# First attention of a Perceiver kernel: blocks taken in pairs, one set of two-bank PSUM tiles, the mask applied on GpSimd after the exponential

## The chip, the cores and the metric

The kernel runs on one core of a Trainium2 chip. The metric is the device time of one execution in microseconds. Before the change it is 784.37 us, the median of three runs (783.34 to 786.42). All times below are microseconds unless marked otherwise.

## What is computed

The network has two layers. A latent array `x` of 128 rows by 256 columns attends to a context of 12,544 rows by 256 columns. Layer 0 is a cross-attention with 4 heads of 64, a gated delta net, and a mixture of experts; layer 1 is a cross-attention with 16 heads of 16 over the same context, a linear attention with decay, and a second mixture of experts. The change is in the first cross-attention and in the loads around it. Cut to that, the reference is:

```
h = layernorm(x)
q = (h @ Wq)                    # 4 heads of 64
k, v = split(context @ Wkv)     # 12544 rows, 4 heads of 64 each
attn = softmax(where(mask, q @ k.T * 64**-0.5, -inf))   # per head, 128 x 12544
x = x + (attn @ v) @ Wo
```

The data are f32, the mask is one byte per entry.

## The kernel before, in words

The context comes in 25 blocks, 24 of 512 rows and one of 256 (`BLOCKS`). All of it stays in SBUF, one tile per block, for layer 1 uses it again. `xattn0_first` (L352) does the first attention. The scores are computed transposed, with the context rows on the partitions, so that the weights need no turning before they are multiplied with the values. One shift per query and head, `nm`, taken from the maximum over the first block, stands in for the running maximum. A second version (`xattn0`, L161), with a running maximum, is executed only when a sum of weights falls out of range; it is not in the executions shown here.

Per block there are four pieces of TensorE work, in an order that is written by hand (`manual_schedule(engines={PE})`, L365; the other engines' orders are made by the scheduler):

- `keys` (L389): for each half m of the 256 key columns, two products of 128x512 into a one-bank PSUM tile `pk`, and a ScalarE copy into `kT` (L399).
- `values` (L401): for each pair of 128-row chunks, four products of 128x256 into a one-bank tile `pv`, and a ScalarE copy into `v` (L412).
- `scores` (L415): per pair of chunks, GpSimd turns the mask bytes into 0 or -1e30 (`mb`, L423) and adds the shift (`shift`, L428); TensorE computes eight products into a two-bank tile `st` (L437); VectorE adds `e = st + shift` (L443), ScalarE takes the exponential in place (L444), VectorE adds e to the running `sums` (L445).
- `weigh` (L448): per e, eight products of v and e into the accumulator `ot` (L455).

In the profile each f32 product shows as two instructions, so a block has 8 `pk`, 16 `pv`, 32 `st` and 32 `ot` instructions.

[...]two tiles of two banks for `st`, three of one bank for everything else (`ps_mm`, L363), one for `ot`. The loop of L502 runs over blocks b: load block b+2, `keys(b)`, `values(b)`, `weigh(b - 1)`, `scores(b)`. After it come six pieces of `filler`, which is work of layer 1's attention (keys and values of the same context, L990 and L1006) used wherever TensorE would wait, and the last `weigh`. The total of filler work is fixed; what is not used in one place is used in a later one.

Ahead of the loop (L461 to L500) stand `keys(0)`, the layer norm of x (L137; its reciprocal root needs two table loads of ScalarE), the query product `pq` (L467) with its scaled copies, the plain scores `sc` of block 0 (L481) with their row maxima on VectorE (L484), `values(0)`, `keys(1)`, and the product `pn` (L495) that spreads the maxima, copied to `nm` (L496).

The loads: SP's queue issues x (L92), Wkv (L368), context block 0, Wq, the mask rows of block 0 (`m0`), block 1, and then blocks and masks as the loop asks for them. GpSimd's queue issues `row`, `col`, the two routers' weights, Wk and Wv of layer 1 (L94, L96, L1489, L1514, L1517) and Wo, with `turned` (L1495, L1496) computed from `row` between them.

Of the kernel before, what the change touches and what calls it, by code (L numbers as in the profile page):

```python
# [11 lines left out]
F32 = mybir.dt.float32  # L12
BF16 = mybir.dt.bfloat16
I32 = mybir.dt.int32
U8 = mybir.dt.uint8
# [56 lines left out]
def network(ctx: ExitStack, tc: tile.TileContext, a: dict, y_out, bad):  # L72
# [18 lines left out]
    x = act.tile([S, D], F32, tag="x", name="x_in")  # L91
    nc.sync.dma_start(x, a["x"])  # L92
    row = const.tile([128, NROW], F32, name="row")
    nc.gpsimd.dma_start(row, a["row"].partition_broadcast(128))  # L94
    col = const.tile([128, NCOL], F32, name="col")
    nc.gpsimd.dma_start(col, a["col"])  # L96
# [21 lines left out]
    def load_ctx(b):  # L118
        r, n = BLOCKS[b]
        nc.sync.dma_start(  # L120
            ctx_blocks[b], a["ctxT"][:, r : r + n].rearrange("(k p) n -> p k n", p=128)
        )
# [229 lines left out]
    def xattn0_first(x, ahead, ok, filler):  # L352
# [4 lines left out]
        with (  # L357
            tc.tile_pool(name="x0_w", bufs=1) as wp,
            tc.tile_pool(name="x0_kv", bufs=2) as kvp,
            tc.tile_pool(name="x0_e", bufs=3) as ep,  # L360
            tc.tile_pool(name="x0_s", bufs=2) as sp,
            tc.tile_pool(name="x0_st", bufs=2, space=PSUM) as ps_st,
            tc.tile_pool(name="x0_mm", bufs=3, space=PSUM) as ps_mm,  # L363
            tc.tile_pool(name="x0_ot", bufs=1, space=PSUM) as ps_ot,
            tc.manual_schedule(engines={PE}),  # L365
        ):
            wkv = wp.tile([128, KC, 2 * D], F32, name="wkv")
            nc.sync.dma_start(wkv, a["L0_xattn_Wkv"].rearrange("(k p) n -> p k n", p=128))  # L368
            load_ctx(0)
            wq = weights(a["L0_xattn_Wq"], D)  # L370
            m0 = sp.tile([S, 512], U8, tag="m0", name="m0", bufs=1)
# [7 lines left out]
            zl = wp.tile([1, 128], BF16, name="zl")  # L379
            nc.gpsimd.memset(zl, 0.0)  # L380
            zr = wp.tile([1, 256], BF16, name="zr")
            nc.gpsimd.memset(zr, 0.0)
# [5 lines left out]

            def keys(b):  # L389
                n = BLOCKS[b][1]  # L390
                kTs[b] = kvp.tile([128, 2, 512], F32, tag="kT", name="kT")[:, :, :n]
                for m in range(2):
                    pk = ps_mm.tile([128, 512], F32, tag="mm", name="pk")
                    for k in range(KC):
                        nc.tensor.matmul(  # L395
                            pk[:, :n], wkv[:, k, m * 128 : (m + 1) * 128], ctx_blocks[b][:, k, :],
                            start=(k == 0), stop=(k == KC - 1),
                        )
                    nc.scalar.copy(kTs[b][:, m, :], pk[:, :n])  # L399

            def values(b):  # L401
                vs[b] = kvp.tile([128, 4, D], F32, tag="v", name="v")
                for c0 in range(0, BLOCKS[b][1] // 128, 2):
                    pv = ps_mm.tile([128, 2, D], F32, tag="mm", name="pv")
                    for c in range(2):
                        rows = slice((c0 + c) * 128, (c0 + c + 1) * 128)
                        for k in range(KC):
                            nc.tensor.matmul(  # L408
                                pv[:, c, :], ctx_blocks[b][:, k, rows], wkv[:, k, D:],
                                start=(k == 0), stop=(k == KC - 1),  # L410
                            )
                    nc.scalar.copy(vs[b][:, c0 : c0 + 2, :], pv)  # L412


            def scores(b):  # L415
                r, n = BLOCKS[b]
                msk = sp.tile([128, 512], U8, tag="msk", name="msk", bufs=3)[:, :n]
                nc.sync.dma_start(msk, a["maskT"][:, r : r + n])
                es[b] = []
                for c0 in range(0, n // 128, 2):  # L420

                    mb = sp.tile([128, 2, S], F32, tag="mb", name="mb")
                    nc.gpsimd.tensor_scalar(  # L423
                        mb, msk[:, c0 * 128 : (c0 + 2) * 128].rearrange("p (c s) -> p c s", c=2),
                        BIG, BIG, ALU.mult, ALU.subtract,
                    )
                    shift = sp.tile([128, 4, 2, S], F32, tag="shift", name="shift")
                    nc.gpsimd.tensor_add(  # L428
                        shift, mb.unsqueeze(1).to_broadcast([128, 4, 2, S]),
                        nm.unsqueeze(2).to_broadcast([128, 4, 2, S]),  # L430
                    )
                    st = ps_st.tile([128, 4, 2, S], F32, tag="st", name="st")
                    for m in range(2):
                        for c in range(2):
                            for q in range(2):
                                rows = slice(q * DH, (q + 1) * DH)
                                nc.tensor.matmul(  # L437
                                    st[:, 2 * q + m, c, :],
                                    kTs[b][rows, m, (c0 + c) * 128 : (c0 + c + 1) * 128], qT[rows, m, :],
                                    start=True, stop=True,  # L440
                                )
                    e = ep.tile([128, 4, 2, S], F32, tag="e", name="e")
                    nc.vector.tensor_add(e, st, shift)  # L443
                    nc.scalar.activation(e, e, AF.Exp)  # L444
                    nc.vector.tensor_add(sums, sums, e)  # L445
                    es[b].append(e)
# [14 lines left out]
            keys(0)  # L461
            hT = layernorm(x, ps_mm, "mm")
            qT = wp.tile([128, 2, S], F32, name="qT")
            for m in range(2):
                pq = ps_mm.tile([128, 512], F32, tag="mm", name="pq")
                for k in range(KC):
                    nc.tensor.matmul(  # L467
                        pq[:, :S], wq[:, k, m * 128 : (m + 1) * 128], hT[:, k, :],
                        start=(k == 0), stop=(k == KC - 1),
                    )  # L470
                nc.scalar.mul(qT[:, m, :], pq[:, :S], DH**-0.5)


            mb0 = sp.tile([S, 512], F32, tag="mb0", name="mb0", bufs=1)
            nc.gpsimd.tensor_scalar(mb0, m0, BIG, BIG, ALU.mult, ALU.subtract)
            mx = sp.tile([S, 4], F32, tag="mx", name="mx")
            for m in range(2):
                sc = ps_st.tile([S, 2, 512], F32, tag="st", name="sc")
                for q in range(2):
                    rows = slice(q * DH, (q + 1) * DH)  # L480
                    nc.tensor.matmul(sc[:, q, :], qT[rows, m, :], kTs[0][rows, m, :], start=True, stop=True)  # L481
                for q in range(2):
                    t = ep.tile([128, 1024], F32, tag="e", name="t")[:, :512]
                    nc.vector.tensor_tensor_reduce(  # L484
                        out=t, in0=sc[:, q, :], in1=mb0, scale=1.0, scalar=-BIG,
                        op0=ALU.add, op1=ALU.max, accum_out=mx[:, 2 * q + m : 2 * q + m + 1],
                    )
            values(0)
            keys(1)
# [4 lines left out]
            pn = ps_mm.tile([128, 4, S], F32, tag="mm", name="pn")  # L494
# [5 lines left out]
            nc.tensor.matmul(ot.rearrange("p m s -> p (m s)"), zl, zr, start=True, stop=False)  # L500

            for b in range(NB):  # L502
                if b + 2 < NB:
                    load_ctx(b + 2)
                if b in ahead:
                    ahead[b]()
                if b > 1:
                    keys(b)
                if b > 0:
                    values(b)  # L510
                    weigh(b - 1, False)
                scores(b)
            filler.into(ps_mm, "mm")
            filler.fill(6)
# [3 lines left out]
            pl = ps_mm.tile([128, 2, S], F32, tag="mm", name="pl")  # L518
# [15 lines left out]
            po = ps_mm.tile([128, 512], F32, tag="mm", name="po")  # L534
# [497 lines left out]
    def weigh1(x, qs, kss, cp, sp, loaded, late):  # L1032
# [4 lines left out]
        with (  # L1037
# [4 lines left out]
            nc.vector.tensor_add(xb, x, row[:S, ROW["bv"]])  # L1042

# [443 lines left out]
    for n, r in enumerate(("L0_ffn_router_w", "L1_ffn_Wg")):  # L1487
        t = const.tile([128, KC, NE], F32, name=f"wr{n}")
        nc.gpsimd.dma_start(t, a[r].rearrange("(k p) n -> p k n", p=128))  # L1489
        wr.append(t)  # L1490
# [4 lines left out]
    nc.gpsimd.tensor_scalar_mul(turned[:, :NE], row[:, ROW["bg"]], -1.0)  # L1495
    nc.gpsimd.tensor_scalar(turned[:, NE:], row[:, ROW["iota"]], -1.0, 64.0, ALU.mult, ALU.add)  # L1496
# [17 lines left out]
    nc.gpsimd.dma_start(wk1, a["L1_xattn_Wk"].rearrange("(k p) n -> p k n", p=128))  # L1514

    wv1 = const.tile([128, KC, D], F32, name="wv1")
    nc.gpsimd.dma_start(wv1, a["L1_xattn_Wv"].rearrange("(k p) n -> p k n", p=128))  # L1517
# [26 lines left out]
    with tc.tile_pool(name="k1", bufs=3) as kp:  # L1544
        filler = Filler(kp)
        if bad is not None:
            ok0 = const.tile([128, 1], F32, name="ok0")
            x = xattn0_first(x, ahead, ok0, filler)
        else:
            x = xattn0(x, ahead)  # L1550
# [128 lines left out]
```

## Time and profile before

| What | us |
|---|---|
| the profiled execution, its own time | 784.51 |
| its span | 782.6 |
| head: 0 to the first transposed scores at 28.0, TensorE busy | 18.1 of 28.0 |
| blocks 0 and 1, 28.0 to 49.7, TensorE busy | 19.0 of 21.7 |
| blocks 2 to 24, 49.7 to 287.6, TensorE busy | 237.9 of 237.9 |
| rest of layer 0, 287.6 to 480, TensorE busy | 189.2 of 192.4 |
| layer 1's attention, 480 to 740, TensorE busy | 258.5 of 260.0 |
| the last layers, 740 to the end, TensorE busy | 27.3 of 42.6 |

The engines are called PE (TensorE), PEld (TensorE's weight loads, which overlap its products), DVE (VectorE), ACT (ScalarE), POOL (GpSimd) and SP. A line of a chain of waits or of a timeline begins with the start and the length in us, then the engine, the source line (in a timeline), the operation, what is written and from what, and how many instructions are taken together. What stands in brackets is the idle time of the engine just before, and what ended it. The busy time of TensorE contains modelled ends of pipelined products, and the times of several instructions together are from the first start to the last end.

### The profile page before, as it was taken

The page shows a single profiled execution, that of the slowest core. Times are in us where ns is not written, and L with a number is a line of the kernel's source. Part 1 is how long each engine was busy: PE and PEld are TensorE (multiplying, and loading weights), DVE is VectorE, ACT ScalarE, POOL GpSimd, SP SyncE. Part 2 cuts the span into 40 slices and gives each one's busy share as a digit, 9 for nine tenths or more (in the row PEclk, how much of TensorE's full clock was granted, in tenths as well). Part 3 has the DMA queues.
Part 4 walks back from the last instruction along what each step waited for, and adds up shares of the span by engine and source line. Part 5 has one row for each costly group of instructions (what it writes and reads, how often), then busy time and mean ns, then how long its engine had stood idle before and what let it go on. Part 6 is the DMA issues. An engine that isn't in the chain of part 4 may idle for free.

```text
span 782.6 us, 23795 instructions
## 1 busy us (share of the span) xinstructions
PE 749.9 (96%) x10821; PEld 558.0 (71%) x10821; DVE 250.5 (32%) x406; ACT 411.2 (53%) x540; POOL 246.4 (31%) x193
## 2 busy tenths in 40 slices
PE   4999999999999999999999999999999999999965
PEld 2667777777777776756668756667888888888852
DVE  0465445654466453983113133000000000000044
ACT  2244334433443334474224533336999999999940
POOL 6597677666776630416012011000000000000000
PEclk9999999999999999999999999999999999999988
DMA  9584000000000002233111345221442222222000
GB/s 291 213 280 172 9 8 4 8 8 8 7 6 6 2 15 84 85 117 123 58 44 41 106 128 134 78 81 58 121 115 74 68 58 74 68 58 72 4 1 12
DMA packets 35742, 56.70 MB, mean 72 GB/s; under 512 B 5760, under 2 KB 11952, under 8 KB 35632
## 3 DMA queue, kind: packets, MB, share of 16 engines
q1 hardware_dynamic: 35232, 54.00, 21.7%
q8 instruction: 87, 1.43, 0.8%
q0 software_dynamic: 400, 1.09, 0.5%
q14 instruction: 23, 0.19, 0.1%
HBM read 42.09 MB, written 12.98 MB: 70 GB/s over the span
## 4 chain that ended last, share of the span: by engine, by line
PE 90%; DVE 3%; ACT 2%; POOL 1%; issue 1%; DMA 1%; SPq 0%; ACTq 0%; DVEq 0%; POOLq 0%
PE st L1067 14%; PE ot L1084 12%; PE pk L395 11%; PE pv L1016 10%; PE pv L408 10%; PE pk L995 10%; PE st L437 6%; PE ot L455 6%; DVE acc L612 1%; DMA ctx<-in_ctxT 1%; POOL shift L428 1%; PE pr L602 1%; PE py L924 1%; PE py L1425 1%; PE pg L732 1%
## 5 line engine op out<-in xcount | busy, mean ns | idle before, releaser
L1073 ACT ACTIVATE e<-st 128x512 f32<-128x512 f32 x196 | 189.7, 1021 | 17.1 <-PE st L1067 15.7
L428 POOL TENSOR_TENSOR shift<-mb,nm 128x1024 f32<-128x1024 f32 x49 | 120.7, 2464 | 73.7 <-DVE e L443 59.3
L1067 PE MATMUL st<-qs,ks 32*128 32x128 f32 x3136 | 115.8, 283 | 0.8 <-ACT e L1073 0.8
L1067 PEld LDWEIGHTS st<-qs,ks 32*128 32x128 f32 x3136 | 96.9, 186 | 21.4 <-ACT e L1073 20.9
L444 ACT ACTIVATE e<-e 128x1024 f32<-128x1024 f32 x49 | 51.8, 1057 | 101.5 <-DVE e L443 100.0
L1084 PE MATMUL ot<-e,ctx 128*17 128x128 f32 x3136 | 104.7, 274 | 0.0
L395 PE MATMUL pk<-ctx,wkv 128*128 128x512 f32 (+1 forms) x200 | 93.7, 613 | 9.3 <-DMA ctx<-in_ctxT 9.3
L443 DVE TENSOR_TENSOR e<-st,shift 128x1024 f32<-128x1024 f32 x49 | 57.9, 1220 | 113.5 <-PE st L437 105.2
L995 PE MATMUL pk<-ctx,wk 128*128 128x512 f32 (+1 forms) x200 | 92.8, 591 | 1.3 <-ACT ctx L1021 1.3
L1016 PE MATMUL pv<-wv,ctx 128*128 128x256 f32 x392 | 92.8, 382 | 0.9 <-ACT kh L1002 0.9
L408 PE MATMUL pv<-wkv,ctx 128*128 128x256 f32 x392 | 89.2, 380 | 1.6 <-ACT kT L399 1.6
L408 PEld LDWEIGHTS pv<-wkv,ctx 128*128 128x128 f32 x392 | 74.2, 190 | 22.3 <-issue 10.0
L445 DVE TENSOR_TENSOR sums<-sums,e 128x1024 f32<-128x1024 f32 x49 | 87.8, 1792 | 4.8 <-ACT e L444 1.2
L1016 PEld LDWEIGHTS pv<-wv,ctx 128*128 128x128 f32 x392 | 72.8, 190 | 20.4 <-issue 10.0
L1084 PEld LDWEIGHTS ot<-e,ctx 128*17 128x17 f32 x3136 | 77.5, 97 | 11.9 <-ACT e L1073 0.3
L423 POOL TENSOR_SCALAR mb<-msk 128x256 f32<-128x256 uint8 x49 | 72.2, 1474 | 4.2
L395 PEld LDWEIGHTS pk<-ctx,wkv 128*128 128x128 f32 x200 | 37.1, 195 | 48.4 <-issue 45.4
L1113 DVE RECIPROCAL den<-pt 128x16 f32<-128x16 f32 x1 | 0.3, 257 | 208.7 <-PE pt L1110 208.7
L1002 ACT ACTIVATE kh<-pk,col 128x512 f32<-128x512 f32 (+1 forms) x50 | 33.9, 678 | 59.0 <-PE pk L995 58.8
L995 PEld LDWEIGHTS pk<-ctx,wk 128*128 128x128 f32 x200 | 36.1, 190 | 31.5 <-issue 26.5
L1021 ACT COPY ctx<-pv 128x512 f32<-128x512 f32 x49 | 28.7, 587 | 54.3 <-PE pv L1016 54.2
L412 ACT COPY v<-pv 128x512 f32<-128x512 f32 x49 | 28.6, 586 | 54.3 <-PE pv L408 54.3
(322 smaller groups left out, 620.3 us busy)
## 6 DMA issues: line engine op xcount, KB each, us to landing
ctx<-in_ctxT SPq DMA_DIRECT2D x24, 512.0 KB, 8.4
kd<-kh SPq DMA_DIRECT2D x48, 256.0 KB, 2.0
ks<-kd SPq DMA_DIRECT2D x192, 64.0 KB, 2.8
w<-in_L_ffn_expert_w SPq DMA_DIRECT2D x4, 512.0 KB, 3.7
ctx<-in_L_ffn_We SPq DMA_DIRECT2D x4, 512.0 KB, 4.7
msk<-in_maskT SPq DMA_DIRECT2D x24, 64.0 KB, 1.9
w<-in_L_attn_Wqk SPq DMA_DIRECT2D x2, 768.0 KB, 9.7
w<-in_L_attn_Wv SPq DMA_DIRECT2D x2, 768.0 KB, 5.1
```

The source lines that it names most:

```text
L395: nc.tensor.matmul(pk[:, :n], wkv[:, k, m * 128 : (m + 1) * 128], ctx_blocks[b][:, k, :], start=(k == 0), stop=(k == KC - 1),)
L408: nc.tensor.matmul(pv[:, c, :], ctx_blocks[b][:, k, rows], wkv[:, k, D:], start=(k == 0), stop=(k == KC - 1),)
L423: nc.gpsimd.tensor_scalar(mb, msk[:, c0 * 128 : (c0 + 2) * 128].rearrange("p (c s) -> p c s", c=2), BIG, BIG, ALU.mult, ALU.subtract,)
L428: nc.gpsimd.tensor_add(shift, mb.unsqueeze(1).to_broadcast([128, 4, 2, S]), nm.unsqueeze(2).to_broadcast([128, 4, 2, S]),)
L443: nc.vector.tensor_add(e, st, shift)
L444: nc.scalar.activation(e, e, AF.Exp)
L445: nc.vector.tensor_add(sums, sums, e)
L995: nc.tensor.matmul(pk, wk1[:, k, m * 128 : (m + 1) * 128], ctx_blocks[b][:, k, :], start=(k == 0), stop=(k == KC - 1),)
L1016: nc.tensor.matmul(pv[:, c, :], ctx_blocks[b][:, k, rows], wv1[:, k, :], start=(k == 0), stop=(k == KC - 1),)
L1067: nc.tensor.matmul(st3[:, j - 1, g, :] if j else st1[:, 0, g, :], kss[b % 3][r, g // 2, g % 2, c * 128 : (c + 1) * 128], qs[r, g, :], star ...
L1073: nc.scalar.activation(e[:, j].rearrange("p j g s -> p (j g s)"), st.rearrange("p j g s -> p (j g s)"), AF.Exp,)
L1084: nc.tensor.matmul(ot[32 * j : 32 * j + DH + 1, g, :], v[:, c, 8 * (g // 2) + 2 * j + g % 2, :], e[:, j, g, :], start=False, stop=(i + 1 = ...
```

## The change

1. Blocks are taken two at a time. For a pair the loop does `values` and `add_up` of the two blocks before, `keys` of both new ones, `weigh` of the two before, and `scores` of both new ones. Context blocks are loaded four and five ahead.
2. PSUM: one pool of three tiles of two banks serves scores, keys, values and everything else in this stage. `keys` writes both halves m into one such tile, `values` both chunk pairs.
3. The mask: the add is now `e = st + nm`; after the exponential, GpSimd multiplies e with the mask as 0 or 1 (`mk`). The additions to `sums` are a function of their own, `add_up`.
4. There are five `e` buffers instead of three, and four mask buffers instead of three.
5. ScalarE's order is now also the written one (`engines={PE, ACT}`).
6. Twenty products of zeros, 128x128 by 128x512 in bf16, whose result is not read, are issued ahead of `keys(0)`. The layer norm's steps are issued around `keys(0)`.
7. Loads: the key half of Wkv comes first, then block 0, then x, Wq, the value half of Wkv, m0, block 1. A function `rest` issues `col` on SP's queue, and `row`, the routers' weights, Wk and Wv of layer 1 on GpSimd's queue, after the computation of the first shift has been issued. `turned` is computed from layer 1's code, and the scheduler puts it after these loads.
8. At the end of the loop three pieces of filler stand between the two `weigh` of the last pair and five before the last one.

The core of the diff:

```
-            tc.tile_pool(name="x0_e", bufs=3) as ep,
-            tc.tile_pool(name="x0_st", bufs=2, space=PSUM) as ps_st,
+            tc.tile_pool(name="x0_e", bufs=5) as ep,
             tc.tile_pool(name="x0_mm", bufs=3, space=PSUM) as ps_mm,
-            tc.manual_schedule(engines={PE}),
+            tc.manual_schedule(engines={PE, ACT}),
+            for _ in range(20):
+                nc.tensor.matmul(spare, zl, zr, start=True, stop=True)
...
+            def two(name):
+                return ps_mm.tile([128, 2, 512], F32, tag="mm", name=name)
             def keys(b):
+                pk = two("pk")
                 for m in range(2):
-                    pk = ps_mm.tile([128, 512], F32, tag="mm", name="pk")
                     for k in range(KC):
                         nc.tensor.matmul(
-                            pk[:, :n], wkv[:, k, m * 128 : (m + 1) * 128], ctx_blocks[b][:, k, :],
+                            pk[:, m, :n], wkv[:, k, m * 128 : (m + 1) * 128], ctx_blocks[b][:, k, :],
                             start=(k == 0), stop=(k == KC - 1),
                         )
-                    nc.scalar.copy(kTs[b][:, m, :], pk[:, :n])
+                    nc.scalar.copy(kTs[b][:, m, :], pk[:, m, :n])
             def values(b):
-                for c0 in range(0, BLOCKS[b][1] // 128, 2):
-                    pv = ps_mm.tile([128, 2, D], F32, tag="mm", name="pv")
+                pv = two("pv")
+                for i in range(BLOCKS[b][1] // 256):
...
-                    nc.scalar.copy(vs[b][:, c0 : c0 + 2, :], pv)
+                    nc.scalar.copy(
+                        vs[b][:, 2 * i : 2 * i + 2, :], pv[:, i, :].rearrange("p (c d) -> p c d", c=2)
+                    )
             def scores(b):
-                    nc.gpsimd.tensor_scalar(
-                        mb, msk[:, c0 * 128 : (c0 + 2) * 128].rearrange("p (c s) -> p c s", c=2),
-                        BIG, BIG, ALU.mult, ALU.subtract,
-                    )
-                    nc.gpsimd.tensor_add(
-                        shift, mb.unsqueeze(1).to_broadcast([128, 4, 2, S]),
-                        nm.unsqueeze(2).to_broadcast([128, 4, 2, S]),
-                    )
-                    st = ps_st.tile([128, 4, 2, S], F32, tag="st", name="st")
+                    st = two("st").rearrange("p q (m c s) -> p (q m) c s", m=2, c=2)
...
-                    nc.vector.tensor_add(e, st, shift)
+                    nc.vector.tensor_add(e, st, nm.unsqueeze(2).to_broadcast([128, 4, 2, S]))
                     nc.scalar.activation(e, e, AF.Exp)
-                    nc.vector.tensor_add(sums, sums, e)
+                    mk = sp.tile([128, 2, S], F32, tag="mk", name="mk", bufs=2)
+                    nc.gpsimd.tensor_scalar(
+                        mk, msk[:, c0 * 128 : (c0 + 2) * 128].rearrange("p (c s) -> p c s", c=2),
+                        1.0, 0.0, ALU.mult, ALU.add,
+                    )
+                    nc.gpsimd.tensor_mul(e, e, mk.unsqueeze(1).to_broadcast([128, 4, 2, S]))
                     es[b].append(e)
+            def add_up(b):
+                for e in es[b]:
+                    nc.vector.tensor_add(sums, sums, e)
...
-            hT = layernorm(x, ps_mm, "mm")
+            hT = layernorm(x, ps_one, "mm", lambda n: keys(0) if n == 4 else None)
...
+            rest()
+            for b in range(0, NB, 2):
+                pair = [b, b + 1] if b + 1 < NB else [b]
+                for c in range(b + 4, min(b + 6, NB)):
+                    load_ctx(c)
+                for c in pair:
+                    if c in ahead:
+                        ahead[c]()
+                if b > 0:
+                    for c in (b - 2, b - 1):
+                        if c > 0:
+                            values(c)
+                        add_up(c)
+                    for c in pair:
+                        keys(c)
+                    weigh(b - 2, False)
+                    if b + 1 == NB:
+                        filler.into(ps_one, "mm")
+                        filler.fill(3)
+                    weigh(b - 1, False)
+                for c in pair:
+                    scores(c)
```

The order of the built program, which the diff alone does not show, for one pair of blocks A and B (two e tiles each, e0 to e3), from its scores to the next pair's:

```
PE    st0 st1 st2 st3 | values A | values B | keys C | keys D | ot e0 e1 e2 e3
DVE   add0 add1  sums(e0)  add2 add3  sums(e1) sums(e2) sums(e3)
ACT   exp0 exp1 exp2 exp3 | v A, v A | v B, v B | kT C, kT C | kT D, kT D
POOL  mul(e0) mk2 mul(e1) mk3 mul(e2) mk0' mul(e3) mk1'
```

`mk0'` and `mk1'` belong to the next pair. The waits that the built program sets on these: each `sums` waits for its `mul`; each `mul` for its `exp`; `ot` for `mul`. PSUM tiles go round in threes: `st3` waits for add0, values A for add1, values B for add2, keys C for add3. Within one values or keys tile, the first product into the second bank waits for ScalarE's copy out of the first bank. The same holds for the two halves of the query product `pq`.

## The prediction

> **What bounds the kernel now.** I read the page first (busy time), then the chain of waits of the first attention, its timeline, and last the windows of the tail. The page says that TensorE is the limit:
>
> ```profile
> ## 1 busy us (share of the span) xinstructions
> PE 749.9 (96%) x10821; PEld 558.0 (71%) x10821; DVE 250.5 (32%) x406; ACT 411.2 (53%) x540; POOL 246.4 (31%) x193
> ```
>
> The chain of waits for 100 to 150 us holds nothing but TensorE work, one block after the other:
>
> ```profile
> 104.57 1.99 PE st L437 x32
> 106.55 3.63 PE pk L395 x8
> 110.18 3.45 PE pv L408 x16
> 113.64 1.90 PE ot L455 x32
> 115.54 1.99 PE st L437 x32
> ```
>
> A block takes 115.54 - 104.57 = 10.97 us, a pair 21.93, without a gap. So a shorter chain on another engine gains nothing here; only less TensorE work does, and every new wait of TensorE costs in full. The timeline of the same block prices the other engines (start, length, engine, line):
>
> ```profile
> 105.78 2.36 DVE L443 TENSOR_TENSOR e<-st,shift 128x1024 f32<-128x1024 f32 x2 [4.87 <-PE st L437]
> ...
> 107.09 2.37 POOL L428 TENSOR_TENSOR shift<-mb,nm 128x1024 f32<-128x1024 f32 x1 [2.81 <-DVE e L443]
> 107.10 2.19 ACT L444 ACTIVATE e<-e 128x1024 f32<-128x1024 f32 x2 [3.80 <-DVE e L443]
> 108.19 3.68 DVE L445 TENSOR_TENSOR sums<-sums,e 128x1024 f32<-128x1024 f32 x2
> ...
> 109.54 1.92 POOL L423 TENSOR_SCALAR mb<-msk 128x256 f32<-128x256 uint8 x1
> ```
>
> GpSimd runs beside TensorE and waits for VectorE there. The first `sums` waits until the running `shift` ends (109.46); the second is not slowed by `mb`, which stretches from 1.07 to 1.92. The minimum of a `sums` is 1.22.
>
> **Fewer changes of tile shape: a gain.** Sixteen products right after a change of shape cost more than later ones: `st` 1.09 alone, 1.99 for 32, so 2 x 1.09 - 1.99 = 0.19 extra; `ot` 2 x 1.02 - 1.90 = 0.14; `pk` 1.92 for the first four instructions, 1.72 for later ones, 0.20. That is 0.54 per block, and a pair pays it once: 21.93 becomes 21.4. Over 12 pairs about -6.5 us. No stage of this size can gain more, as TensorE was never idle in it.
>
> **Two-bank tiles: a wait inside every keys and values tile.** In the built order, the products into a tile's second bank wait for ScalarE's copy of the first bank, because the wait belongs to the tile. Before, each half had its own tile and the copy ran beside the next one's products. A half is 1.72. ScalarE starts 0.04 after it (v copies: half ends 111.91, copy 111.95), takes 0.59, and TensorE follows 0.04 later: 0.67 idle, and then a refill of 0.20 (values after the copy that ended at 45.80 took 1.99, elsewhere 1.73). So 0.87 per tile. The Trainium skill ("PSUM — Partial Sum Buffer", "Summary: rules for kernel authors") asks of a read beside running products only that it be in a different bank, which the halves are: by the page no wait is needed and the four tiles would cost nothing; by the built order they wait, at 0.87. No row of before shows such a tile. The engines obey the semaphores of the program, so I take 0.87. Cover: none; the next work of TensorE stands behind the waiting product.
>
> **ScalarE in written order, and one sum in VectorE's queue: the long wait.** The first of these four tiles waits for more. ScalarE's copy of values' first half is queued behind the four exponentials of the pair, the fourth needs VectorE's fourth add, and VectorE's order is add, add, sum of the first e, add, add. That sum waits for GpSimd's mask product. Counted from the end of the last `ot`: 1.21 to the first add (105.78 - 104.57); add 1.22 gives 2.43; 0.10 and exp 1.06 give 3.59; 0.09 and the mask product give 6.05; 0.08 and the sum 1.23 give 7.36; two adds give 9.78; 0.10 and exp 1.06 give 10.94; the copy 0.59 gives 11.53; 0.04 more: 11.57. The mask product is not in the trace; `shift` has its size, engine and inputs of broadcast kind, 2.37 (bounds: 2.07, twice the 1.036 of a 512-wide product with broadcast at L648, to the 3.37 of a contended `shift`). The sum is 1.23 (bounds 1.22 to the row's maximum of 3.29). TensorE has meanwhile done four `st` tiles (3.78) and half the values (1.92) by 5.70, so it idles 5.87.
>
> The rest of a pair: second half 1.92 to 13.49; values of the second block 1.72 + 0.67 + 1.92 to 17.8; two keys tiles the same to 26.42; 64 `ot` 3.66 to 30.1. GpSimd's four rounds (1.92 + 2.37 each, 3.68 to about 20) and the four copies stay ahead of that. A pair is 30.1 against 21.93: +8.15. Behind the stalled TensorE stands the whole pair.
>
> **The mask.** mk (1.07) and product (2.37) replace mb (1.07) and shift (2.37) on GpSimd: no less work. Before it lay ahead of the add with GpSimd waiting 59.3 us in all for VectorE; now it lies in the chain above, counted there. The add reads `nm` from SBUF in place of `shift`: 1.22 as before.
>
> **The clock.** TensorE now idles 5.87 us in every pair. The windows of the tail show what such a pause does (length, then busy times of PE, PEld, DVE, ACT, POOL, then the granted clock):
>
> ```profile
> 745.00:748.00 3.00, 1.05 (x17) 0.46 (x7) 1.19 (x5) 1.34 (x4) 0.00 (x0) 1.00 0.00 0
> 748.00:751.00 3.00, 0.77 (x3) 0.80 (x4) 1.73 (x7) 0.50 (x2) 0.00 (x0) 0.72 0.00 0
> 751.00:754.00 3.00, 3.00 (x15) 2.75 (x14) 0.31 (x2) 0.77 (x5) 0.00 (x0) 0.50 0.00 0
> 754.00:757.00 3.00, 3.00 (x18) 2.79 (x17) 2.15 (x6) 1.32 (x5) 0.00 (x0) 0.64 0.00 0
> ```
>
> TensorE paused 3.56 us (746.67 to 750.23); the missing clock (0.28, 0.50, 0.36 of 3 us, doubled) is 6.84 us at half speed, some 5.9 of them after work resumed at 750.23. A second dip at 766 to 772 us (0.56 and 0.87) is 3.4 us. The Trainium skill ("TensorE: Matmul & The Clock Gate", Part 1) states free-running windows of about 3.4 us, half clock after an idle one, full after a busy one: by it one such window at half costs 1.7 us, by the first row 5.9 / 2 = 3.0. I take the mean of the two dips, 4.7 us at half, 2.1 us lost, in each of 12 pairs: +25. Bounds: 0 if the pause is not long enough, 36 if each is like the first dip.
>
> **The head.** The first keys took 6.73 us from 9.34, later ones 3.63: a cold start costs 3.1. Twenty unread products of bf16 128x512 begin once GpSimd has set its zeros, near 2.3 us (the five small steps before them take 1.3 in the timeline, and no DMA stands ahead now). The one bf16 product in the trace (`ot` by zl, 256 wide) shows one instruction where each f32 product shows two, so I estimate 0.42 cold (half of the 0.85 spacing of cold f32 instructions) and 0.21 warm. With the 6.1 us that the first keys ran cold, they end near 9.7 (8.3 to 11.5). The context block, before landing at 9.2 behind 1.15 MB, now stands behind 0.77 MB and is there. Keys then run warm: 1.72 + 0.67 + 1.92, ending at 14.0 and not 15.9. The query product has the same wait (+0.5), values and keys of the first blocks too (+1.8), so the first scores start at 28.4 and not 27.96. The first pair, with one values tile, takes 25.8: the third block's scores begin at 54.2, before at 49.74, with equal work done.
>
> Moved steps: five DMAs on GpSimd's queue (0.73 to 0.77 each to issue) and `turned`, which waits for one of them (6.3 to land), now stand behind mb0, ahead of the first mk; the engine idled 12.3 us there until 28.70, which hides them. If that cover failed the first product would be late by the difference. SP's queue takes one small DMA more, and masks and blocks are loaded further ahead: nothing waits for them after 60 us. x lands third, and its chain to h (3.0 us) still ends before 14.0.
>
> **Sum.** Ten pairs at 30.1 and a last one of 27.0 (one half-sized keys tile, three filler products between) give 328 from the third block's scores to the last one's; before it was 287.57 - 49.74 = 237.8, with 0.9 less work done: +89.3. Head and first pair +4.5. Together +93.8; with the clock +119. Against the profiled execution's 784.51 (span 782.6; median 784.37): 903.
>
> **The rivals.**
> - The clock holds, 784.5 + 94 = 878. For it: the page shows 0.99 over the whole span and shapes change without harm. Against: 3.56 us were enough once. Chance 0.2.
> - The clock falls more deeply (3 us or more lost a pair, or the sum meets a contended GpSimd, up to +2 a pair): 915 to 940. Chance 0.15.
> - The sum does not hold up the adds (GpSimd's product quicker, or VectorE served otherwise): the fourth exp ends near 7.2, TensorE idles 2.1, a pair takes 26.4 and the whole 784.5 + 93.8 - 12 x 3.7 = 834. Against it: the order is written in the program. Chance 0.04.
> - Faster: copies arrive before TensorE asks for them, that is, the waits between a tile's banks cost nothing. Place: the four second halves of a pair; price: 0; then 6.5 us of shapes and some 3 us of the cold start remain, 775. It decides at a pair of 21.9: all waits of a pair must stay below 0.5 us, less than one copy of 0.59. Chance 0.02. No change: 0.01.
> - As reckoned, 885 to 925: 0.58.
>
> The range 872 to 935 leaves out 834, 775 and the far end of the deep dips. A measurement of this kernel can tell about 0.5% from no change.
>
> **What would show it.** In the changed profile: a pair of scores every 30 to 33 us; idle time before the values' products put down to the v copy, near 6 us each for the first block of a pair and 0.7 for the others; the granted clock below 1 in the body, 0.9 or so; `sums` just ahead of the third add. I am wrong if TensorE's busy share stays at 96%, if the second halves start right after the first, or if the third add starts before the mask product ends.

## The result, and the profile after

The changed kernel takes 907.06 us, the median of four runs (906.54 to 907.21), against 785.0 for the kernel before on the same chip (783.34 to 786.42): a ratio of 1.155, with a 95% interval of 1.153 to 1.157. Its profiled execution took 906.54 with a span of 904.8 and a mean granted clock of 0.948 (before 0.992).

From the page of the changed kernel: the busy times, the granted clock in 40 slices, and the chain of waits by engine.

```profile
PE 787.0 (87%) x10841; PEld 575.1 (64%) x10841; DVE 221.4 (24%) x406; ACT 412.9 (46%) x540; POOL 234.2 (26%) x192
...
PEclk9889889889889988989999999999999999999988
...
PE 55%; issue 22%; POOL 19%; ACT 2%; DVE 1%; POOLq 0%; ACTq 0%; DVEq 0%
```

TensorE went from 96% busy to 87%, and its busy time still rose by 37 us, only 6 of them the unread products of the head: it idles, and its products also take longer. The clock row shows where: below full speed in the first half, which is the first attention, as well as in the last layers, where it was so before. The last line would make GpSimd a culprit. It isn't: GpSimd is busy for 26% of the span, less than before. The chain has walked back along GpSimd's own queue, where a mask product waits for TensorE's next scores ("issue"), and so it misses what TensorE waits for. The timeline of one pair shows that (start, length, engine, line; in brackets the idle time ahead and what ended it):

```profile
151.43 3.84 PE L436 MATMUL st<-qT,kT 64*128 64x128 f32 x64
152.64 2.35 DVE L442 TENSOR_TENSOR e<-st,nm 128x1024 f32<-128x1024 f32 x2 [14.33 <-PE st L436]
...
155.10 2.36 POOL L449 TENSOR_TENSOR e<-e,mk 128x1024 f32<-128x1024 f32 x1 [16.52 <-ACT e L443]
155.20 1.99 PE L416 MATMUL pv<-wkv,ctx 128*128 128x256 f32 x8
157.49 1.23 DVE L454 TENSOR_TENSOR sums<-sums,e 128x1024 f32<-128x1024 f32 x1 [2.50 <-POOL e L449]
...
158.63 2.35 DVE L442 TENSOR_TENSOR e<-st,nm 128x1024 f32<-128x1024 f32 x2
...
159.95 2.19 ACT L443 ACTIVATE e<-e 128x1024 f32<-128x1024 f32 x2 [3.80 <-DVE e L442]
...
162.04 0.57 ACT L420 COPY v<-pv 128x512 f32<-128x512 f32 x1
162.66 6.62 PE L416 MATMUL pv<-wkv,ctx 128*128 128x256 f32 x16 [5.46 <-ACT v L420]
...
170.02 1.99 PE L416 MATMUL pv<-wkv,ctx 128*128 128x256 f32 x8 [0.73 <-ACT v L420]
...
184.45 3.84 PE L436 MATMUL st<-qT,kT 64*128 64x128 f32 x64
```

Read it as one chain: the mask product ends at 157.46, the sum behind it at 158.72, and with it (the records of neighbours on VectorE overlap by 0.09) begin the third and fourth adds; then follow the fourth exponential, the copy of values' first half, and at 162.66 TensorE's second half. TensorE idled 5.46 us, and 0.73 at each of the three other tile halves. The pair took 184.45 - 151.43 = 33.02. The neighbouring pairs alternate between about 31.9 and 33.0; ten of them, from 54.40 to 379.06, have a mean of 32.47 (before: 21.93).

The 16 products at 162.66 took 6.62 where the same number takes 3.72 elsewhere. Windows of the changed kernel around them (window, its length, busy times of PE, PEld, DVE, ACT and POOL, then the granted clock, and last the DMA share and GB/s):

```profile
158.34:161.75 3.41, 0.00 (x0) 0.00 (x0) 3.06 (x4) 1.73 (x2) 3.32 (x3) 1.00 0.00 0
161.75:165.17 3.42, 2.51 (x6) 2.06 (x7) 0.81 (x1) 0.86 (x2) 3.39 (x2) 0.50 0.08 19
165.17:168.58 3.41, 3.41 (x9) 2.69 (x9) 1.23 (x1) 0.59 (x1) 3.35 (x2) 0.50 0.00 0
```

I cut the windows where the clock changes. After one without any product the clock is at half for two windows of 3.415 us, 5.9 us of it in work. All twelve pairs have such a dip, each of 6.83 us (starts at 35.46, 62.77, 96.90, ...: always 8, 9 or 10 times 3.415 apart).

The span in terms, with what the prediction gave each:

| Stretch | predicted | measured |
|---|---|---|
| to the first scores | 28.4 | 26.50 |
| first pair | 25.8 + 2.1 | 27.90 |
| ten pairs | 10 x (30.1 + 2.1) = 322 | 324.66 |
| last pair | 27.0 + 2.1 | 28.43 |
| from the last scores to the end | 495.1 - 0.9 | 497.31 |
| span | 901.6 | 904.8 |

Here 495.1 is what the kernel before takes from its last scores (287.5) to its end (782.6), and 0.9 the filler that the change has by then already done.

### The profile page after: what moved, and what is told of

It reads as the page before. It is cut to its first block, busy times and chain, and to the rows that moved or that the text cites. A ratio compares the mean times of both kernels' runs of the same rounds, so it can differ in the third digit from the quotient of the medians.

```text
span 904.8 us, 23889 instructions
## 1 busy us (share of the span) xinstructions
PE 787.0 (87%) x10841; PEld 575.1 (64%) x10841; DVE 221.4 (24%) x406; ACT 412.9 (46%) x540; POOL 234.2 (26%) x192
## 4 chain that ended last, share of the span: by engine, by line
PE 55%; issue 22%; POOL 19%; ACT 2%; DVE 1%; POOLq 0%; ACTq 0%; DVEq 0%
PE st L1099 12%; POOL e L449 12%; PE ot L1116 10%; PE pv L1046 9%; PE pk L1025 9%; POOL mk L445 7%; PE pv L416 1%; PE pr L632 1%; PE pk L403 1%; PE py L954 1%; PE py L1457 1%; PE spare L370 1%; PE pg L762 1%; PE pout L928 1%; PE pyt L813 1%
## 5 line engine op out<-in xcount | busy, mean ns | idle before, releaser
L416 PE MATMUL pv<-wkv,ctx 128*128 128x256 f32 x392 | 121.8, 471 | 74.3 <-ACT v L420 74.3
L449 POOL TENSOR_TENSOR e<-e,mk 128x1024 f32<-128x1024 f32 x49 | 115.1, 2349 | 209.5 <-ACT e L443 194.9
L416 PEld LDWEIGHTS pv<-wkv,ctx 128*128 128x128 f32 x392 | 90.3, 239 | 102.3 <-ACT v L420 83.9
L1099 PEld LDWEIGHTS st<-qs,ks 32*128 32x128 f32 x3136 | 96.8, 186 | 21.4 <-ACT e L1105 21.2
L442 DVE TENSOR_TENSOR e<-st,nm 128x1024 f32<-128x1024 f32 x49 | 57.7, 1218 | 170.5 <-PE st L436 170.5
L454 DVE TENSOR_TENSOR sums<-sums,e 128x1024 f32<-128x1024 f32 x49 | 60.0, 1225 | 100.4 <-POOL e L449 100.4
L445 POOL TENSOR_SCALAR mk<-msk 128x256 f32<-128x256 uint8 x49 | 68.3, 1394 | 4.1
L407 ACT COPY kT<-pk 128x512 f32<-128x512 f32 (+1 forms) x50 | 28.9, 578 | 80.3 <-PE pk L403 80.3
L1025 PEld LDWEIGHTS pk<-ctx,wk 128*128 128x128 f32 x200 | 36.0, 190 | 28.4 <-issue 24.0
## 6 DMA issues: line engine op xcount, KB each, us to landing
w<-in_L_attn_Wv SPq DMA_DIRECT2D x2, 768.0 KB, 12.8
```

Of the source, the lines that this page charges most:

```text
L416: nc.tensor.matmul(pv[:, i, c * D : (c + 1) * D], ctx_blocks[b][:, k, rows], wkv[:, k, D:], start=(k == 0), stop=(k == KC - 1),)
L442: nc.vector.tensor_add(e, st, nm.unsqueeze(2).to_broadcast([128, 4, 2, S]))
L445: nc.gpsimd.tensor_scalar(mk, msk[:, c0 * 128 : (c0 + 2) * 128].rearrange("p (c s) -> p c s", c=2), 1.0, 0.0, ALU.mult, ALU.add,)
L449: nc.gpsimd.tensor_mul(e, e, mk.unsqueeze(1).to_broadcast([128, 4, 2, S]))
L1025: nc.tensor.matmul(pk, wk1[:, k, m * 128 : (m + 1) * 128], ctx_blocks[b][:, k, :], start=(k == 0), stop=(k == KC - 1),)
L1099: nc.tensor.matmul(st3[:, j - 1, g, :] if j else st1[:, 0, g, :], kss[b % 3][r, g // 2, g % 2, c * 128 : (c + 1) * 128], qs[r, g, :], star ...
```

## The experiments

The kernel before, run beside each group, took 784.56, 786.13 and 785.41.

**The copies behind both halves.** The changed kernel with ScalarE's two copies of a tile issued after all of the tile's products:

```
                 for m in range(2):
                     for k in range(KC):
...
+                for m in range(2):
                     nc.scalar.copy(kTs[b][:, m, :], pk[:, m, :n])
```

and the same in `values` and for `pq`.

> In keys, values and the query product the copies are issued after both halves of the two-bank tile, so the second bank's products wait for nothing; the sum of the first e still stands ahead of the third add. My theory (the waits inside the tiles are the bulk, the long one starting with the sum): TensorE does all of values A without a stop and then waits for the third add, which ends 8.4 after the first st starts, against 7.4: about 1.1 idle a pair, no dip of the clock, a pair of 22.6, and 786 us (783 to 790). Rival, the mask product on GpSimd sits in the chain to ot and sets the pair: no change of the pair's length, 895 to 907.

Measured: 788.12, ratio 1.004 (1.002 to 1.006). TensorE's timeline:

```profile
165.30 3.72 PE L417 MATMUL pv<-wkv,ctx 128*128 128x256 f32 x16 [0.98 <-DVE e L444]
```

A pair is 22.63. Values A now run through; the sum still stands ahead of the third add, and what is left of it is 0.98 us before values B, which need a tile that the third add empties. So of the 122 us between the two kernels 119 (907.06 - 788.12) needed the wait inside the tiles.

**The sums behind the adds.** The changed kernel with VectorE's order also the written one, so that the four adds of a pair come before its sums:

```
-            tc.manual_schedule(engines={PE, ACT}),
+            tc.manual_schedule(engines={PE, ACT, DVE}),
```

> VectorE also in written order: the four adds of a pair first, then its four sums; the copies inside the tiles as changed. My theory: the fourth exp ends near 7.2 after the first st starts and not near 10.6, so the long wait shrinks from 5.46 to about 2.1, the three short ones of 0.73 stay, a pair falls from 32.4 to 26.6 and the time to 837 us; up to 860 if a pause of 2.1 still lowers the clock. Rival, the sum is harmless because GpSimd's products are the bound: about 907.

Measured: 834.6, ratio 1.063 (1.061 to 1.065), a pair 26.38. TensorE's timeline:

```profile
161.98 3.72 PE L417 MATMUL pv<-wkv,ctx 128*128 128x256 f32 x16 [1.74 <-ACT v L421]
166.43 1.99 PE L417 MATMUL pv<-wkv,ctx 128*128 128x256 f32 x8 [0.73 <-ACT v L421]
```

The long pause falls from 5.46 to 1.74, and with it all dips of the clock but one. The prediction had 834 for this case, as a rival.

**Both** of these edits in one kernel.

> Both edits. My theory: no wait of TensorE is left in a pair, which takes 21.4 (before: 21.93), and the shorter head stays: 773 us (769 to 778). Rival, the mask product ends too late for ot of the fourth e once nothing else holds TensorE up (3.65 + 4 x 2.35 + 3 x 1.44 = 17.4 against 20.5 for TensorE by my reckoning): a pair of 22.5 or more and 785 us or above.

Measured: 775.17, ratio 0.988 (0.986 to 0.990); once more in the third group, 774.06, ratio 0.985 (0.984 to 0.987). TensorE's timeline:

```profile
106.79 3.84 PE L439 MATMUL st<-qT,kT 64*128 64x128 f32 x64
110.56 7.17 PE L418 MATMUL pv<-wkv,ctx 128*128 128x256 f32 x32
117.57 7.03 PE L404 MATMUL pk<-ctx,wkv 128*128 128x512 f32 x16
...
128.18 2.06 PE L439 MATMUL st<-qT,kT 64*128 64x128 f32 x32
```

No brackets: TensorE never waits, and a pair takes 21.39, 0.54 less than before. Pairs, two-bank tiles and the mask on GpSimd are all still in; the loss came from two orders.

**The clock.** The changed kernel with unread products of zeros in the long pause of every pair, ahead of values' second half; the computation is unchanged. The diff is the one with 25; the others have 9, 14 and 18.

```
                 for i in range(BLOCKS[b][1] // 256):
+                    if i == 1 and b in (1, *range(2, NB, 2)):
+                        for _ in range(25):
+                            nc.tensor.matmul(spare, zl, zr, start=True, stop=True)
```

> The changed kernel with 25 unread bf16 products put into the long pause, between the two banks of the first values tile of each pair; the result is as before, and the wait itself stays. My theory: the clock no longer falls, the products fit into the pause of 5.46 (25 x 0.216 = 5.4), a pair falls from 32.4 to about 30.0, 878 us (872 to 886). Rival, the granted clock in the records has no effect on the time, or the slow products after the pause have another cause: 907 or more.

Measured with 25: 879.82, ratio 1.121 (1.119 to 1.123), a pair 30.11, no dip.

> The changed kernel with 9 unread products placed in the long pause of each pair (25 of them kept the clock up, 879.82 us), so that the pause of 5.46 us is left at about 3.5. Nothing else is different, so the time tells how long a pause lowers the clock. If only a pause of more than about 3.4 us that fills a whole fixed window counts: the dips go almost everywhere, about 880. If a window that is mostly idle is enough: dips in most pairs, 2 us each, about 900. In between: about 890.

Measured with 9: 904.47, ratio 1.151 (1.149 to 1.153), a pause of 3.52. That is near the 900 of the second case and far from the first: every pair but the first has a dip. Windows cut at the changes of the clock:

```profile
156.37:159.78 3.41, 0.77 (x4) 0.15 (x2) 3.06 (x4) 1.76 (x2) 3.32 (x3) 1.00 0.00 0
159.78:163.20 3.42, 2.54 (x6) 2.09 (x7) 0.81 (x2) 0.83 (x2) 3.36 (x2) 0.50 0.07 19
163.20:166.61 3.41, 3.41 (x9) 2.69 (x9) 1.20 (x1) 0.59 (x1) 3.38 (x2) 0.50 0.00 0
```

A window with 0.77 us of products lowered the clock, one with 2.54 did not raise it, a full one did.

> The changed kernel with 14 unread products in the long pause of each pair, which leaves about 2.4 us of it (9 products left 3.52 and the clock fell to half in every pair, for 3.42 or 6.83 us; 25 left nothing but the 0.73 ones and it never fell). My theory from those traces: the clock is set at the ends of windows of 3.415 us that run on freely, and it falls when a window held under about 1 us of products. With 2.4 us of pause a window can hold as little as 1.0, and only when its edges lie just so: dips in at most 4 of the 12 pairs, 880 to 887. Rival, that a pause of 2 us or more is enough wherever it lies: dips everywhere, about 900.

Measured with 14: 886.7, ratio 1.128 (1.125 to 1.130), a pause of 2.44, and five dips of 3.42, not at most four. Two windows of it, the first with a dip behind it, the other without:

```profile
123.19:126.60 3.41, 0.97 (x5) 0.36 (x4) 2.79 (x3) 2.59 (x3) 3.32 (x3) 1.00 0.00 0
...
92.50:95.91 3.41, 1.38 (x7) 0.41 (x5) 3.05 (x3) 2.23 (x3) 3.32 (x3) 1.00 0.00 0
```

> The changed kernel with 18 unread products in the long pause, which leaves about 1.6 us: no window of 3.415 us can hold less than 1.8 us of products. My theory: no dip in the first attention, 880 (878 to 882), the same as with 25. Rival: about 900.

Measured with 18: 879.94, ratio 1.120 (1.119 to 1.122), a pause of 1.57, no dip. TensorE's timeline, the 16 products behind the pause at full speed (3.72 where the changed kernel took 6.62):

```profile
154.08 3.72 PE L419 MATMUL pv<-wkv,ctx 128*128 128x256 f32 x16 [1.57 <-ACT v L423]
```

So without dips the changed kernel takes 880 and with them 907, at the same waits; and what decides is how much work a window holds, not whether the pause fills it.

**Only the mask, in the kernel before.** Shift and mask leave the add as in the change; blocks, tiles and orders stay.

```
-                    nc.gpsimd.tensor_scalar(
-                        mb, msk[:, c0 * 128 : (c0 + 2) * 128].rearrange("p (c s) -> p c s", c=2),
-                        BIG, BIG, ALU.mult, ALU.subtract,
-                    )
...
-                    nc.gpsimd.tensor_add(
-                        shift, mb.unsqueeze(1).to_broadcast([128, 4, 2, S]),
-                        nm.unsqueeze(2).to_broadcast([128, 4, 2, S]),
-                    )
...
-                    nc.vector.tensor_add(e, st, shift)
+                    nc.vector.tensor_add(e, st, nm.unsqueeze(2).to_broadcast([128, 4, 2, S]))
                     nc.scalar.activation(e, e, AF.Exp)
...
+                    nc.gpsimd.tensor_scalar(
+                        mk, msk[:, c0 * 128 : (c0 + 2) * 128].rearrange("p (c s) -> p c s", c=2),
+                        1.0, 0.0, ALU.mult, ALU.add,
+                    )
+                    nc.gpsimd.tensor_mul(e, e, mk.unsqueeze(1).to_broadcast([128, 4, 2, S]))
                     nc.vector.tensor_add(sums, sums, e)
```

> The kernel before with one part of the change alone: the mask's shift goes out of the add, and the exponentials are multiplied by the mask on GpSimd instead, with the sums behind that. My theory: the product (2.35 us) stands in the chain from scores to weighted values, but in a single block of the kernel before it ends about 9.9 us after the scores begin, where TensorE comes to read it at about 10: the blocks stay at 10.97 and the time at 785 (783 to 790). Rival, that the mask product on GpSimd costs by itself: at least 0.5 us in each of 23 blocks, 795 or more.

Measured: 792.81, ratio 1.009 (1.007 to 1.011): between the two cases, and outside both. The blocks in the middle stay at 10.97 (116.57 to 127.54), so the rival's cost per block is not there. What my expectation left out is the two places where less TensorE work than elsewhere lies between a block's scores and its weights. In the middle these are keys and values, 7.1 us; behind the first block there are only values (3.7), behind the last full one the keys and values of the half-sized block (3.9). TensorE's timeline of the first:

```profile
33.38 1.09 PE L451 MATMUL ot<-e,v 128*64 128x128 f32 x16 [0.39 <-POOL e L440]
37.20 1.14 PE L451 MATMUL ot<-e,v 128*64 128x128 f32 x16 [2.73 <-POOL e L440]
38.27 3.59 PE L427 MATMUL st<-qT,kT 64*128 64x128 f32 x32
```

The mask product stands bare there, and the pause lowers the clock (the scores take 3.59 for 2.06). The other place has the same two pauses (0.38 and 2.73) and the same dip. The third block's scores are 1.1 later than before, the next layer's first keys 6.0, the span 8.0. Of the remaining 2.0, 1.66 lie behind layer 1's attention (38.92 against 37.26), where this execution was at half clock for 18.6 us and the one before for 12.8.

**The unread products ahead of the first keys**, in the version with both re-orderings: none (the lines go), and ten:

```
-            for _ in range(20):
+            for _ in range(10):
                 nc.tensor.matmul(spare, zl, zr, start=True, stop=True)
```

> The version with both re-orderings (775.17 us) without its 20 unread products ahead of the first keys. What is on record: those products hold TensorE to about 7.7 us, and the first key projection ends at 11.72; its inputs have landed by about 5.7 us, and in the kernel before the same projection, cold, took 6.7. My theory: without them keys begin at 5.3 and end at about 12.0, so the products are worth almost nothing: 775 (774 to 777). Rival, the warm-up is worth the whole cold start, 3 us: 778.

Measured without: 773.31, ratio 0.984 (0.983 to 0.986), 0.7 below the expected range. The keys of the first block in TensorE's timeline:

```profile
5.31 6.01 PE L401 MATMUL pk<-ctx,wkv 128*128 128x512 f32 x8 [5.31 <-DMA ctx<-in_ctxT]
```

They end at 11.3, with 20 products at 11.7; the first scores come at 23.55 without and at 23.95 with them. The twenty are worth nothing: they end the cold start, but hold TensorE for as long as they save.

> The version with both re-orderings with 10 unread products in place of 20. My theory, that the 20 run on past the landing of the first inputs and so give back what they save: keys begin near 6.3 and end near 10.6 where they ended at 11.72, so about 774 (773 to 775). Rival, that fewer products leave TensorE cold: keys take longer and the time is 775 to 777.

Measured with ten: 771.73, ratio 0.983 (0.981 to 0.984), 1.3 below the expected range.

```profile
2.00 3.81 PE L371 MATMUL spare<-zr,zl 128*128 128x512 bf16 x10 [2.00 <-POOL zr L368]
5.65 3.60 PE L404 MATMUL pk<-ctx,wkv 128*128 128x512 f32 x8
```

The keys start at 5.65, 0.3 after their inputs had landed in the version without unread products (5.31), run at full speed, and the first scores come at 21.47. Ten and twenty on one chip, again:

> The version with both re-orderings and 20 unread products once more (775.17 in the first call), next to the one with 10 on the same chip, because the spread between calls (the kernel before read 784.6 in one and 786.1 in the other) is as large as what 20, 10 and no products differ by. First scores at 24.0 against 21.5 in the traces: if that is kept, 774.5 beside 772 for ten.

> The version with both re-orderings and 10 unread products once more (771.73), on the same chip as the one with 20: 2.5 us below it if the earlier first scores are kept to the end, 772. If the end's own pauses eat that, within 1 us of it.

Measured: 774.06 and 772.01, ratios 0.985 (0.984 to 0.987) and 0.983 (0.981 to 0.985). The first scores came at 21.47 and 21.90 with ten, at 23.95 and 25.00 with twenty, so the head is 2.5 and 3.1 us shorter; the whole time is about 2 shorter, with intervals that overlap a little. The version with both orders and ten products is the fastest here: 1.7% below the kernel before.

## Why the prediction held, point by point

- **TensorE is the bound, and each of its waits costs in full.** Right. From the first scores to the last the changed kernel takes 380.99, and 251.72 with both waits taken away, which is 129.3 less; the whole time is 131.9 less, and the other 2.6 are the head (26.50 against 23.95).
- **Fewer changes of shape, 21.93 to 21.4.** Right: 21.39.
- **0.87 per two-bank tile.** Right in kind: the wait is there as the built order has it, and is gone with the copies last. It was put too low, for it costs about 1.0. The idle time is 0.73 where 0.67 was reckoned. Without the sum ahead of the adds a pair has 1.74 + 3 x 0.73 = 3.93 of idle time and is 26.38 - 21.39 = 4.99 longer; the other 1.06 are four refills of 0.27, where 0.20 was taken. The two figures that the prediction gives for the refill, 1.99 and 1.73, make 0.26.
- **The long wait, 5.87.** Right link by link, and 5.46 in size. The chain's start is as reckoned (first add 1.21 after the scores begin, third add at 7.2 where 7.36 was reckoned), the two adds together take 2.35 and not 2.42, and so on to 11.23 and not 11.57. What the prediction did not say: this wait reaches TensorE only through the wait inside the tile. With the tile's wait gone 0.98 was left; with the sum gone 1.74. Either cause alone costs little or half; the prediction's sum is right only because both are there.
- **A pair at full clock, 30.1.** 30.11 where the clock was held. That it fits so closely is luck: the long wait was put 0.4 too high, the four tiles together 0.4 too low. The rival at 878, the same sum without the clock, is what the two versions with held clock show (879.82 and 879.94). The rival at 834 was measured as 834.6 once its condition was made: no outcome of this change, but a right price. The rival at 775 was not: it asked only that the waits between a tile's banks cost nothing, and with these gone 788.12 was measured, because the sum still held up values B by 0.98. The 775.17 came when the sum was moved as well.
- **The clock, 2.1 a pair.** 32.47 - 30.11 = 2.36; in all 907.06 - 879.94 = 27 for 25 reckoned. The 2.1 is a slip of the sum: 4.7 us at half clock lose 4.7 / 2 = 2.35, in twelve pairs 28. And the size is a mean of two dips of the tail that are two different things, one window at half and two. The changed kernel has two in every pair; the loss still comes out near the mean because 0.7 to 3.3 us of each dip lie in the pause, which was luck. By the Trainium skill's page ("TensorE: Matmul & The Clock Gate", Part 1), half clock follows an idle window; the windows here have its length, 3.415, but need not be idle: 0.77 and 0.97 us of products were not enough. Had only whole idle windows counted, the pause of 3.52 would have been nearly free, and it cost nearly as much as that of 5.46.
- **The mask.** Right that GpSimd's work is off the path but for the first product of a pair. `mk` took 1.44 beside the sums (1.92 was taken): each of the 47 in the pairs starts 0.05 after a sum has begun and ends 0.27 after that sum. The two without a sum beside them (17.71 and 18.09) took 0.40. The product took 2.35, the sum 1.23 each time. In the kernel before, the mask alone costs 0.9%, at both ends of the loop.
- **The head, 28.4.** Wrong by 1.9, in one term: the unread products were to begin near 2.3 and end near 9.7, with 6.1 us of them cold, as long as the first keys ran cold in the kernel before. They began at 2.00, and the keys behind them at 7.65. The starts of neighbours are 0.43 apart at first and 0.22 from 4.74 on: cold for 2.7 us, not 6.1. Keys ended at 12.19, not 14.0. In part that is the chance of this execution. In eight other profiled executions with twenty the keys began at 8.08 to 9.17, after 3.6 to 5.8 us of cold products. The twenty in the changed kernel, and in the second execution with both orders:

```profile
2.00 5.81 PE L370 MATMUL spare<-zr,zl 128*128 128x512 bf16 x20 [2.00 <-POOL zr L367]
...
2.00 7.33 PE L371 MATMUL spare<-zr,zl 128*128 128x512 bf16 x20 [2.00 <-POOL zr L368]
```

- **The rest, 495.1 - 0.9.** Measured 497.31. Of the 2.2 above 495.1, 2.1 lie between the last scores and the last product of layer 1's attention: 459.95 against 457.84, with the same busy time (452.6 and 453.0) and 2.6 more idle. The prediction took the moved filler at its length. Filler used before the last scores could be lacking in layer 0's later waits, but that does not explain it alone: the other versions of the change, with the same filler, took 457.7 to 460.3 there. The cause stays open.

By the table the errors are -1.9 in the head, +2.7 in the ten pairs, -0.7 in the last pair and +3.1 behind, together +3.2: the whole is closer than its parts because they cancel in part.

## What to carry to other kernels

When two halves of one tile are filled and emptied in turn, issue the readers after all writers, or take two tiles: otherwise the second half inherits whatever the first half's reader is queued behind. Follow that queue over every engine before trusting an order: here one unimportant sum, placed by the scheduler ahead of an add, was worth 72 us (907.06 - 834.6) while TensorE waited for a copy inside a tile, and 13 (788.12 - 775.17) once the copies came last. Where TensorE must pause, price the clock too, and ask how little work lies in any window of 3.4 us, and not only how long the pause is.

## What the runs showed of the hardware

- The granted clock changed only at multiples of 3.415 us. In the first attention it fell after all windows with up to 1.26 us of products and once after one with 1.56 (sums behind adds, 265.18), and held after all others, the lowest with 1.38; once low, it rose after windows with 3.1 or more and stayed low after others, the fullest with 2.7. What decides between 1.3 and 1.6 is not settled.
- In the last layers, whose products have other shapes, the same sums do not decide: the clock fell after windows with up to 2.0 us (sums behind adds, 824.96) and stayed low after one counted as busy throughout (mask only, 771.99 to 775.40). A threshold in busy time from one stage is not one for another.
- The pauses of the last layers cost differently from one execution to the next. Behind layer 1's attention the two profiled executions of the kernel with ten unread products had 13.3 and 18.6 us at half clock, and took 37.3 and 38.9. That is nearly as much as the head's versions differ by.
- The windows 0 to 4 us of the profile show a granted clock of 1.00 because the trace has no record of the clock there. Its first record begins at 4.74 in the changed kernel and at 15.46 in the kernel before, just where the products' spacing halves (0.43 to 0.22, and the first keys' 0.85 to 0.43): the end of the cold start. The last window before it held 2.74 us of products in the changed kernel. In the kernel before a window with 2.71 did not end it, and the next, full one did.
